# Layer 0's first keys issued ahead of what waits for other transfers, and GpSimd's bias add in the second heads issued behind a key layout

## The chip, the cores and the metric

One core of a Trainium2 chip runs the whole program in one launch. The metric is the device time of one execution in microseconds, as the median of several executions. Engines are named as in the profile: PE is TensorE (PEld its weight load), DVE is VectorE, ACT is ScalarE, POOL is GpSimd, and SP is SyncE, which here only issues transfers. ACT issues transfers too, in order with its own computing.

## The reference

The reference is a chain of four layers on 2048 tokens of width 128 (32 sequences of 64), float32 throughout. Each layer adds a cross attention and then a feed-forward to the residual stream x. Cut to what matters here:

```python
# layer 0, attention: 16 heads of 64; queries from the 64 latents, keys from context and latents
kv_in = concat([layer_norm(ctx, g1, b1), layer_norm(layernorm(x), g2, b2)], axis=1)
q = l @ Wq;  k, v = split(kv_in @ Wkv)
out = softmax(q k^T / 8) v @ Wo;         x = x + out
# layer 0 feed-forward, layer 1 attention, layer 1 mixture of experts (top 2 of 8, two iterations)
# layers 2 and 3, attention: 16 heads of 8 with masks, keys and values from ctx_1024
out = softmax(q k^T / sqrt(8) + mask) v @ Wo + bo;   x = x + out
# layer 2 feed-forward: quantized weights and activations; layer 3: top 2 of 8 experts
```

## The kernel before, in words

**Tiles and groups.** The tokens lie as 16 tiles of 128 in four groups `K.x[g]` of four tiles. Layer 0's attention goes over eight inputs q = 0..7; each holds four batches, with 64 context tokens on partitions 0 to 63 and 64 latents on partitions 64 to 127 (`kv_tok`).

**The folding.** No queries or keys are made. `l0_products` multiplies each head's query and key weights into one 128x128 matrix (`A`, kept as a high and a low part by `take_A`), and the value and output weights into `N`. `l0_project` multiplies the normed latents (`latT`) by `A` in three matmuls per head (`mm3`, L236) into `G`; the scores are then `G` times `kvT` (L445). The products are made in two halves `hf` of eight heads each; projections n = 0..3 need the first half of A, n = 4..7 the second.

**An input's way.** `l0_load` fetches `kv_tok` in two transfers, the context half issued by SP and the latent half by ACT, into two buffers, so the tokens of input q + 2 wait until input q's are read for the last time. `l0_inputs` then runs moments (L154, L155), ln_rs, a power on GpSimd (L161), the normalization (L183), gamma and beta (L403, L404: on VectorE for q = 0, on GpSimd else), four PE transposes (L408), an ACT copy to `kvT` (L409), and splits into high and low parts: `latT_hi` (L213), `latT_lo` (L218), `tokp_hi`, `tokp_lo`. In the code `l0_inputs(1)` and the products come after `l0_inputs(0)`.

**Units.** `l0_unit` takes one (q, tile, half, batch) through scores, softmax, transposes (L465), values (L236 into `c_ps`) and, at the end of a tile, the sum over heads with `N` (L479), which is added to `K.x` (L480). Each unit also makes one projection of the next input. `interleave` keeps three units in flight and, beside them, steps of the tasks in `K.behind`: the weights of the middle layers and each group's further work.

**Who sets the order.** Every engine runs its instructions in the order given. The order is made at build time by a planner that simulates the program with costs of its own and issues what is ready by its clock, in program order where several are. `in_turn` gives it edges that only fix the order of issue of two instructions; `issue_after` does so for all that a block issues on the engine of one instruction. Such an edge brings no waiting of its own between instructions of one engine.

**Constants.** `constants` makes the identity and a column of -0.5; `later_constants`, the first step of the middle weights, makes a bfloat16 and a rounded identity, half of `cols` (all bias columns, one transfer of 24.5 KB, L299), the pair mask and a ranking row. The four loads of `K.x` and the load of `cols` stand in the code after the products.

**The heads of layers 2 and 3.** `heads_xattn(K, i, ...)` runs for i = 0 (layer 2) and i = 1 (layer 3, the second heads). `heads_tile` lays out one tile's keys on GpSimd (`kb`, L1249, two buffers), makes the scores with a mask matmul and a key matmul (L1262, L1263), softmax (L1264 to L1266), transposes (L1273), values (L1283), and at the end of a group turns the output (L204), adds the output bias to `x` on GpSimd (L1309), multiplies by Wo (L1315) and adds to `x` on VectorE (L1316). Three tiles are in flight, so the next group's first tiles are begun before a group's end. For i = 0 the bias add of a group but the last has an edge behind the latest key layout; for i = 1 it has none. `queries` reads x through `hqn` (L183) before the bias may be added. `keep_warm` issues matmuls whose results nobody reads.

Of the kernel before, what the change touches and what calls it, by code (L numbers as in the profile page):

```python
# [4 lines left out]


# [3 lines left out]

# [8 lines left out]
F32 = mybir.dt.float32  # L19
# [5 lines left out]
ALU = mybir.AluOpType  # L25
# [121 lines left out]
def ln_moments(K, pool, xg, own=""):  # L147

    nc = K.nc
    n = xg.shape[1]  # L150
    st = pool.tile([P, n, 6], F32, name="ln_st")
    mv = pool.tile([P, n, 2], F32, name=f"ln_mv{own}")
    for t in range(n):
        nc.vector.bn_stats(st[:, t, :], xg[:, t, :])  # L154
        nc.vector.bn_aggr(mv[:, t, :], st[:, t, :])  # L155
    return mv
# [51 lines left out]
def split(K, pool, src, name, engine=None, bufs=None, after=None):  # L208

    nc = K.nc  # L210
    hi = pool.tile(list(src.shape), F32R, name=f"{name}_hi", bufs=bufs)
    lo = pool.tile(list(src.shape), F32R, name=f"{name}_lo", bufs=bufs)
    first = nc.scalar.copy(hi, src) if isinstance(K, Later) else nc.vector.tensor_copy(hi, src)  # L213
    if after:
        in_turn(K, [after, first])
    if not isinstance(K, Later):
        K.mark = first
    (engine or nc.gpsimd).tensor_tensor(lo, src, hi.bitcast(F32), ALU.subtract)  # L218
    return hi, lo


# [61 lines left out]
def constants(K, pool):  # L283

    nc = K.nc
    K.ident = pool.tile([P, P], F32, name="ident")
    make_identity(nc, K.ident)
    K.neghalf = pool.tile([P, 1], F32, name="neghalf")
    nc.vector.memset(K.neghalf, -0.5)


def later_constants(K, pool):
    nc = K.nc
    K.identb = pool.tile([P, P], BF16, name="identb")
    nc.vector.tensor_copy(K.identb, K.ident)
    K.identr = pool.tile([P, P], F32R, name="identr")
    nc.vector.tensor_copy(K.identr, K.ident)
    K.half = pool.tile([P, NCOL], F32, name="half_cols")
    nc.vector.tensor_scalar(K.half, K.cols, 0.5, None, ALU.mult)  # L299

    K.pair_mask = pool.tile([P, GT, P], BF16, name="pair_mask")
    nc.vector.memset(K.pair_mask, NEG)
    for b in range(2):
        nc.vector.memset(K.pair_mask[b * S : (b + 1) * S, :, b * S : (b + 1) * S], 0.0)

    K.rank = pool.tile([P, 8], F32, name="rank")
    for e in range(8):
        nc.vector.memset(K.rank[:, e : e + 1], float(8 - e))
# [7 lines left out]
N_TAGS = "2n"  # L316


def l0_products(K, out, left, right, hf, tags=("s", "t")):


    ps = [bank(K, tag, [P, 4, P]) for tag in tags]
    for j in range(4):
        for r in range(2):
            rows = slice(r * S, (r + 1) * S)
            K.nc.tensor.matmul(ps[r][:, j, :], left[rows, 4 * hf + j, :], right[rows, 4 * hf + j, :], start=True, stop=True)
    for r in range(2):
        out(ps[r], hf, r)


def l0_xattn(K):


    nc, tc, ins = K.nc, K.tc, K.ins
    with (
        tc.tile_pool(name="l0x_w", bufs=1, reuse_waits="tile") as wp,
        tc.tile_pool(name="l0x_g", bufs=2, reuse_waits="tile") as gp,
        tc.tile_pool(name="l0x_t", bufs=L0_BUFS, reuse_waits="tile") as tp,
    ):
        C = SimpleNamespace(gp=gp, tp=tp, tok={}, keys={}, G={})  # L340

        C.A = tuple(wp.tile([P, 16, P], F32R, name=f"A_{n}") for n in ("hi", "lo"))
        C.N = wp.tile([P, 16, P], F32, name="N")
        with tc.tile_pool(name="first", bufs=1, side="right", reuse_waits="tile") as first:
            l0_load(K, C, 0)
            w = {n: first.tile([P, 8, P], F32, name=n) for n in ("WqT", "WkT", "WvT", "Wo")}
            from_dram = {n: ins[f"L0_xattn_{n}"].rearrange("(c p) d -> p c d", p=P) for n in w}
            half = [slice(4 * hf, 4 * hf + 4) for hf in range(2)]
            gains = wp.tile([P, 2, P], F32, name="gains")
            K.kv_gamma, K.kv_beta = gains[:, 0, :], gains[:, 1, :]  # L350
            for hf in range(2):
                nc.sync.dma_start(w["WqT"][:, half[hf], :], from_dram["WqT"][:, half[hf], :])
                nc.scalar.dma_start(w["WkT"][:, half[hf], :], from_dram["WkT"][:, half[hf], :])
                if hf == 0:
                    nc.sync.dma_start(gains, ins["gains"])
            l0_load(K, C, 1)
            nc.sync.dma_start(w["WvT"], from_dram["WvT"])
            nc.scalar.dma_start(w["Wo"], from_dram["Wo"])
            heads = lambda t, hf, r: t.rearrange("p (c r) d -> p r c d", r=2)[:, r, half[hf], :]

            def take_A(ps, hf, r):
                hi, lo = (heads(a, hf, r) for a in C.A)
                scale = 1.0 / math.sqrt(64.0)
                nc.scalar.activation(hi, ps, AF.Copy, scale=scale)
                nc.vector.scalar_tensor_tensor(lo, ps, scale, hi.bitcast(F32), ALU.mult, ALU.subtract)

            l0_inputs(K, C, 0)
            for hf in range(2):
                l0_products(K, take_A, w["WqT"], w["WkT"], hf)
                for n in range(4 * hf, 4 * hf + 4):  # L370
                    l0_project(K, C, 0, n, "gn"[n % 2])
            l0_inputs(K, C, 1)

            with tc.issue_after(K.projected.ins):
                for hf in range(2):
                    l0_products(K, lambda ps, hf, r: nc.scalar.copy(heads(C.N, hf, r), ps), w["WvT"], w["Wo"], hf, N_TAGS)
        for g in range(NG):
            K.x[g] = K.load(K.const, f"x{g}", [P, GT, P], K.tokens(ins["x"], g))
        K.cols = K.load(K.const, "cols", [P, NCOL], ins["cols"])
        mid_begin(K)  # L380
        units = [(q, t, hf, b) for q in range(8) for t in range(2) for hf in range(2) for b in range(2)]
        interleave(K, (Task(l0_unit(K, C, *u)) for u in units), L0_DEPTH, L0_LAG, L0_RATE)


def l0_load(K, C, q):
    tok = C.tok[q] = C.gp.tile([P, GT, P], F32, name="kv_tok")
    for rows, name, queue in ((slice(0, S), "ctx_1024", K.nc.sync), (slice(S, P), "x", K.nc.scalar)):
        batches = K.ins[name].rearrange("(b s) d -> s b d", s=S)
        queue.dma_start(tok[rows, :, :], batches[:, GT * q : GT * (q + 1), :])


def l0_inputs(K, C, q):

    nc, gp = K.nc, C.gp
    tok = C.tok[q]
    mv = ln_moments(K, gp, tok)
    rs = gp.tile([P, GT], F32, name="ln_rs")
    nc.vector.tensor_scalar(rs[0:S, :], mv[0:S, :, 1], EPS, None, ALU.add)
    nc.vector.tensor_scalar(rs[S:P, :], mv[S:P, :, 1], 1.0 + EPS, EPS * EPS, ALU.mult, ALU.add)
    ln_apply(K, tok, tok, mv, rsqrt(K, gp, rs, "ln_rstd"))  # L400
    full = [P, GT, P]
    engine = nc.vector if q == 0 else nc.gpsimd
    engine.tensor_tensor(tok, tok, K.kv_gamma.unsqueeze(1).to_broadcast(full), ALU.mult)  # L403
    engine.tensor_tensor(tok, tok, K.kv_beta.unsqueeze(1).to_broadcast(full), ALU.add)  # L404
    kvT = gp.tile(full, F32, name="kvT", bufs=3)
    ps = bank(K, "1", full)
    for b in range(GT):
        nc.tensor.transpose(ps[:, b, :], tok[:, b, :], K.ident)  # L408
    nc.scalar.copy(kvT, ps)  # L409
    latp = split(K, gp, kvT[:, :, S : 2 * S], "latT", nc.vector)  # L410
    tokp = split(K, gp, tok, "tokp", bufs=3)
    C.keys[q] = (kvT, latp, tokp)

# [14 lines left out]
def l0_unit(K, C, q, t, hf, b):  # L428
# [5 lines left out]
    G = C.G[q]  # L434
    if n == 0 and q + 2 < 8:
        l0_load(K, C, q + 2)
    if n == 2 and q + 2 < 8:
        l0_inputs(K, C, q + 2)
    if (hf, b) == (0, 0):
# [604 lines left out]
HEAD_BLOCKS = ("L2", "L3")  # L1044
WARM = ((0, 0, 0, 0), (0, 0, 2, 4))
WARM_END = 2


def heads_constants(K, pool):
# [185 lines left out]
def heads_tile(K, C, g, t):  # L1235
# [17 lines left out]
    if C.i:  # L1253
        in_turn(K, [K.l2bo_step, step])
    K.kb_step = step
    yield
    nm = C.gp.tile([P, 16], F32, name="nm", bufs=HX_BUFS)
    e = C.ep.tile([P, 16, S], F32, name="e")
# [50 lines left out]
    step = nc.gpsimd.tensor_tensor(xg, xg, K.hbo[C.i].unsqueeze(1).to_broadcast([P, n, P]), ALU.add)  # L1309
    if C.i == 0 and g < NG - 1:  # L1310
        in_turn(K, [K.kb_step, step])
    yield
    ps = bank(K, QN[C.i], [P, n, P])
    for t in range(n):
# [53 lines left out]
def keep_warm(K, ps, n, after=None):  # L1368

    cols = ps.shape[-1]  # L1370
    moving = K.masks[1].rearrange("p h k -> p (h k)") if len(K.masks[1].shape) == 3 else K.masks[1]
    for _ in range(n):
        step = K.nc.tensor.matmul(ps, K.identb, moving[:, :cols], start=True, stop=True)
        if after is not None:
            in_turn(K, [after, step])
        after = step
    return after
# [361 lines left out]
```

## Time and profile before

| | |
|---|---|
| median of 3 runs | 907.39 us (906.65 to 907.55) |
| the profiled execution, its own time | 907.62 us |
| its span in the profile | 905.9 us |
| PE / DVE / ACT / POOL busy | 821.4 / 732.4 / 563.0 / 328.3 us |
| transfers | 13.73 MB, mean 15 GB/s |

The profile lists busy time, not waiting. A row of the order of time reads: start, duration, engine, line, operation, what it writes and reads, its shape, and in brackets how long the engine was idle before it and what it waited for. DMA queues are SPq and ACTq, by the engine that issues. Matmul durations include a tail that overlaps with the next, so the rate of TensorE is read from the spacing of starts. The windows view gives busy time per engine for stretches of the span.

### The profile page before, as it was taken

How to read it: one execution, taken by the hardware profiler on the slowest of the kernel's cores; microseconds unless marked ns; L12 is line 12 of the kernel's file. 1: busy time of each engine (PE TensorE's matmuls, PEld its weight loads, DVE VectorE, ACT ScalarE, POOL GpSimd, SP SyncE). 2: the span in 40 equal slices, each digit the busy share in tenths (PEclk: the TensorE clock that was granted, in tenths of full speed). 3: DMA queues.
4: the chain of work that ended last, by engine and by line, in shares of the span. 5: the costliest groups of instructions: out<-in, count | busy, mean ns of one | idle time of the engine just before them, and what ended most of it. 6: DMA issues, size and time to landing. Idle time of an engine off the chain costs nothing.

```text
span 905.9 us, 15766 instructions
## 1 busy us (share of the span) xinstructions
PE 821.4 (91%) x5859; PEld 671.2 (74%) x5868; DVE 732.4 (81%) x1877; ACT 563.0 (62%) x1093; POOL 328.3 (36%) x300
## 2 busy tenths in 40 slices
PE   4999999999999988899999799898999779898995
PEld 3989989979988876787787688684676447566663
DVE  5879799798698687877678877789788778789878
ACT  3676685676676599587687768564544484345443
POOL 3764574343243251511040310015474303435342
PEclk9999999999999999999999999999999999899998
DMA  8312000000000000000000000000000000000000
GB/s 191 106 36 59 13 2 12 13 1 1 13 1 1 1 13 0 15 14 21 1 1 1 1 1 1 0 25 1 1 2 1 1 1 1 1 1 1 13 13 24
DMA packets 22670, 13.73 MB, mean 15 GB/s; under 512 B 3009, under 2 KB 21953, under 8 KB 22593
## 3 DMA queue, kind: packets, MB, share of 16 engines
q1 hardware_dynamic: 18320, 10.62, 4.3%
q10 hardware_dynamic: 4272, 2.10, 0.9%
q8 instruction: 46, 0.75, 0.3%
q14 instruction: 32, 0.25, 0.1%
HBM read 11.66 MB, written 1.05 MB: 14 GB/s over the span
## 4 chain that ended last, share of the span: by engine, by line
PE 50%; DVE 25%; ACT 15%; POOL 3%; issue 3%; DMA 2%; SPq 1%; ACTq 0%; DVEq 0%; POOLq 0%
PE c_ps L918 7%; PE g_ps L479 4%; PE s_ps L1263 4%; PE s_ps L445 4%; PE g_ps L236 4%; PE c_ps L236 3%; PE g_ps L1283 2%; PE c_ps L1273 2%; PE s_ps L236 2%; PE t_ps L465 2%; PE t_ps L236 2%; ACT L941 2%; DVE mh_lo L895 1%; ACT L936 1%; DVE m L893 1%
## 5 line engine op out<-in xcount | busy, mean ns | idle before, releaser
L461 POOL TENSOR_TENSOR e<-e,rs 128x512 f32<-128x512 f32 x64 | 67.0, 1058 | 91.7 <-DVE rs L460 52.8
L161 POOL TENSOR_TENSOR ln_rstd<-ln_rs,neghalf 128x4 f32<-128x4 f32 (+1 forms) x38 | 40.8, 1073 | 144.8 <-DVE ln_rs L169 137.5
L1249 POOL TENSOR_TENSOR kb<-hk,head 128x1024 f32<-128x1024 f32 x32 | 63.7, 1993 | 74.2 <-PE s_ps L1263 58.9
L445 PE MATMUL s_ps<-kvT,G 128*128 128x128 f32 x512 | 71.7, 277 | 0.5 <-DVE e L451 0.5
L1263 PE MATMUL s_ps<-kb,hq 128*128 128x512 f32 x128 | 67.3, 609 | 2.1 <-ACT hq L1232 1.9
L445 PEld LDWEIGHTS s_ps<-kvT,G 128*128 128x128 f32 x512 | 65.8, 192 | 4.1 <-DVE e L451 1.9
L918 PE MATMUL c_ps<-mh_hi,w2e_hi 128*128 128x512 f32 x160 | 61.8, 426 | 4.5 <-ACT be L936 2.7
L479 PE MATMUL g_ps<-N,Ct 128*128 128x128 f32 x512 | 62.1, 276 | 1.1 <-ACT G L425 0.7
L479 PEld LDWEIGHTS g_ps<-N,Ct 128*128 128x128 f32 x512 | 60.1, 192 | 2.5 <-ACT G L425 1.3
L1266 ACT ACTIVATE e<-e 128x1024 f32<-128x1024 f32 x32 | 34.0, 1061 | 40.6 <-DVE e L1265 38.1
L1264 DVE TENSOR_REDUCE nm<-s_ps 128x8 f32<-128x512 f32 x64 | 43.7, 683 | 16.0 <-PE s_ps L1263 15.6
L1274 ACT COPY hpT<-c_ps 128x512 f32<-128x512 f32 x64 | 35.1, 589 | 34.2 <-PE c_ps L1273 33.9
L469 DVE TENSOR_TENSOR pT_lo<-t_ps,pT_hi 128x512 fp32r<-128x512 f32 x64 | 43.4, 683 | 13.5 <-ACT pT_hi L468 11.3
L918 PE MATMUL c_ps<-mh_hi,w2e_lo 128*128 128x512 f32 x160 | 51.9, 401 | 0.0
L895 DVE TENSOR_TENSOR mh_lo<-m,mh_hi 128x1024 fp32r<-128x1024 f32 x32 | 40.4, 1263 | 13.9 <-ACT mh_hi L894 12.9
L473 ACT COPY Ct<-c_ps 128x512 f32<-128x512 f32 x64 | 38.4, 600 | 21.2 <-PE c_ps L236 16.4
L918 PE MATMUL c_ps<-mh_lo,w2e_hi 128*128 128x512 f32 x160 | 49.4, 404 | 0.5 <-DVE mh_lo L895 0.5
L425 ACT COPY G<-g_ps 128x512 f32<-128x512 f32 x60 | 35.9, 598 | 21.4 <-PE g_ps L236 18.0
L452 ACT ACTIVATE e<-e 128x512 f32<-128x512 f32 x56 | 35.4, 638 | 20.8 <-DVE e L451 20.5
L1283 PEld LDWEIGHTS g_ps<-hv,hpT 128*64 128x64 f32 x1024 | 33.5, 137 | 19.3 <-issue 7.4
L447 DVE TENSOR_REDUCE nm<-s_ps 128x4 f32<-128x512 f32 x64 | 42.9, 679 | 5.0 <-PE s_ps L445 4.7
L468 ACT CAST pT_hi<-t_ps 128x512 fp32r<-128x512 f32 x64 | 38.1, 598 | 13.3 <-PE t_ps L465 7.3
(524 smaller groups left out, 2651.8 us busy)
## 6 DMA issues: line engine op xcount, KB each, us to landing
kv_tok<-in_x ACTq DMA_DIRECT2D x8, 128.0 KB, 3.3
kv_tok<-in_ctx SPq DMA_DIRECT2D x8, 128.0 KB, 2.9
x<-in_x SPq DMA_DIRECT2D x4, 256.0 KB, 8.3
ctx<-in_ctx SPq DMA_DIRECT2D x4, 256.0 KB, 3.4
w2e_raw<-in_L_ffn_expert_w SPq DMA_DIRECT2D x1, 768.0 KB, 4.4
out<-x SPq DMA_DIRECT2D x3, 256.0 KB, 2.3
WkT<-in_L_xattn_WkT ACTq DMA_DIRECT2D x2, 256.0 KB, 5.3
WqT<-in_L_xattn_WqT SPq DMA_DIRECT2D x2, 256.0 KB, 5.2
```

The lines of the kernel that those rows point to most:

```text
L236: step = K.nc.tensor.matmul(ps, w[a], x[b], start=start and i == 0, stop=stop and i == 2)
L445: nc.tensor.matmul(ps[:, j, :], G[:, bb, h : h + 2, :].rearrange("p h s -> p (h s)"), kvT[:, bb, :], start=True, stop=True)
L447: K.mark = nc.vector.tensor_reduce(nm, ps, AX.X, ALU.max, negate=True)
L461: nc.gpsimd.tensor_tensor(e, e, rs.unsqueeze(2).to_broadcast([P, 4, P]), ALU.mult)
L469: nc.vector.tensor_tensor(lo, ps, hi.bitcast(F32), ALU.subtract)
L479: nc.tensor.matmul(ps, Ct[:, h, :], C.N[:, h, :], start=(h == 0), stop=(h == 15))
L895: nc.vector.tensor_tensor(lo, m, hi.bitcast(F32), ALU.subtract)
L918: nc.tensor.matmul(ps, K.w2p[part][:, 2 * n + i, cols], x[:, i, :, :], start=first, stop=last)
L1249: step = nc.gpsimd.tensor_tensor(kb, K.hk[C.i][g][:, :, t, :].unsqueeze(2).to_broadcast(full), K.head.unsqueeze(1).unsqueeze(3).to_broadca ...
L1263: nc.tensor.matmul(ps, hq[:, half, t, :, :].rearrange("p b s -> p (b s)"), kb[:, half, :, :], start=False, stop=True)
L1264: nc.vector.tensor_reduce(nm[:, heads], ps, AX.X, ALU.max, negate=True)
L1283: values = nc.tensor.matmul(po[b * S : (b + 1) * S, j, :, :].rearrange("p r d -> p (r d)"), pT[:, j, b * S : (b + 1) * S], K.hv[g][:, 2 * ...
```

## The change

In the start:

- the bfloat16 identity and the pair mask are made in `constants`, with the first instructions;
- eight warming matmuls of 128x512 stand first on TensorE, and six more behind the first half of the products, which now comes in the code ahead of `l0_inputs(0)`; the second half of the products is issued behind the last of input 0's transposes (`K.turn0`);
- the moments of input 1 and `half_cols` are issued on VectorE behind input 0's `latT_lo` (`K.lat0`);
- `cols` is loaded ahead of WvT; the four loads of x move into the first unit, behind the tokens of input 2, and both halves of those tokens are issued by SP.

In the heads: for i = 1 each bias add is issued behind the latest second tile's key layout (`C.kb_second`). At the end of group g < 3 that is the second tile of group g + 1, which is already begun; in group 3 it is group 3's own. The warming matmuls take the pair mask as their moving operand everywhere.

```diff
 def split(...):
-    (engine or nc.gpsimd).tensor_tensor(lo, src, hi.bitcast(F32), ALU.subtract)
+    K.split_end = (engine or nc.gpsimd).tensor_tensor(lo, src, hi.bitcast(F32), ALU.subtract)
...
 def later_constants(K, pool):
-    nc.vector.tensor_scalar(K.half, K.cols, 0.5, None, ALU.mult)
+    in_turn(K, [K.lat0, nc.vector.tensor_scalar(K.half, K.cols, 0.5, None, ALU.mult)])
...
 def l0_products(K, out, left, right, hf, tags=("s", "t"), after=None):
+            if after is not None:
+                in_turn(K, [after, step])
...
             l0_load(K, C, 0)
+            keep_warm(K, bank(K, "1", [P, 512]), WARM_START)        # WARM_START = 8
...
             l0_load(K, C, 1)
+            K.cols = K.load(K.const, "cols", [P, NCOL], ins["cols"])
             nc.sync.dma_start(w["WvT"], from_dram["WvT"])
...
+            step = l0_products(K, take_A, w["WqT"], w["WkT"], 0)
+            keep_warm(K, bank(K, "g", [P, 512]), 6, step)
             l0_inputs(K, C, 0)
             for hf in range(2):
-                l0_products(K, take_A, w["WqT"], w["WkT"], hf)
+                if hf:
+                    l0_products(K, take_A, w["WqT"], w["WkT"], hf, after=K.turn0)
...
-        for g in range(NG):
-            K.x[g] = K.load(K.const, f"x{g}", [P, GT, P], K.tokens(ins["x"], g))
-        K.cols = K.load(K.const, "cols", [P, NCOL], ins["cols"])
...
 def l0_load(K, C, q):
-        queue.dma_start(tok[rows, :, :], batches[:, GT * q : GT * (q + 1), :])
+        K.tok_step = (queue if q != 2 else K.nc.sync).dma_start(tok[rows, :, :], batches[:, GT * q : GT * (q + 1), :])
...
 def l0_inputs(K, C, q):
-    mv = ln_moments(K, gp, tok)
+    with K.tc.issue_after(K.lat0.ins) if q == 1 else nullcontext():
+        mv = ln_moments(K, gp, tok)
...
+    if q == 0:
+        K.turn0, K.lat0 = turn, K.split_end
...
 def l0_unit(K, C, q, t, hf, b):
         l0_load(K, C, q + 2)
+        if q == 0:
+            for g in range(NG):
+                x = K.x[g] = K.const.tile([P, GT, P], F32, name=f"x{g}")
+                in_turn(K, [K.tok_step, K.nc.sync.dma_start(x, K.tokens(K.ins["x"], g))])
...
 def heads_tile(K, C, g, t):
+    if t == 1:
+        C.kb_second = step
...
+    if C.i:
+        in_turn(K, [C.kb_second, step])
...
 def keep_warm(K, ps, n, after=None):
-    moving = K.masks[1].rearrange("p h k -> p (h k)") if len(K.masks[1].shape) == 3 else K.masks[1]
+    moving = K.pair_mask.rearrange("p t k -> p (t k)")
```

More of the change, by code (lines that the diff above doesn't have):

```diff
@@ L7 @@
 import math
-from contextlib import ExitStack
+from contextlib import ExitStack, nullcontext
 from types import SimpleNamespace
@@ L287, in constants @@
     make_identity(nc, K.ident)
+    K.identb = pool.tile([P, P], BF16, name="identb")
+    nc.vector.tensor_copy(K.identb, K.ident)
+    K.pair_mask = pool.tile([P, GT, P], BF16, name="pair_mask")
+    nc.vector.memset(K.pair_mask, NEG)
+    for b in range(2):
+        nc.vector.memset(K.pair_mask[b * S : (b + 1) * S, :, b * S : (b + 1) * S], 0.0)
     K.neghalf = pool.tile([P, 1], F32, name="neghalf")
@@ L293, in later_constants @@
     nc = K.nc
-    K.identb = pool.tile([P, P], BF16, name="identb")
-    nc.vector.tensor_copy(K.identb, K.ident)
     K.identr = pool.tile([P, P], F32R, name="identr")
@@ L298, in later_constants @@
     K.half = pool.tile([P, NCOL], F32, name="half_cols")
[L299 to L304, printed above, removed]
+    in_turn(K, [K.lat0, nc.vector.tensor_scalar(K.half, K.cols, 0.5, None, ALU.mult)])
     K.rank = pool.tile([P, 8], F32, name="rank")
@@ L316, with l0_products @@
 N_TAGS = "2n"
-def l0_products(K, out, left, right, hf, tags=("s", "t")):
+def l0_products(K, out, left, right, hf, tags=("s", "t"), after=None):
     ps = [bank(K, tag, [P, 4, P]) for tag in tags]
@@ L325, in l0_products @@
             rows = slice(r * S, (r + 1) * S)
-            K.nc.tensor.matmul(ps[r][:, j, :], left[rows, 4 * hf + j, :], right[rows, 4 * hf + j, :], start=True, stop=True)
+            step = K.nc.tensor.matmul(ps[r][:, j, :], left[rows, 4 * hf + j, :], right[rows, 4 * hf + j, :], start=True, stop=True)
+            if after is not None:
+                in_turn(K, [after, step])
     for r in range(2):
         out(ps[r], hf, r)
+    return step
 def l0_xattn(K):
@@ L407, in l0_inputs @@
     for b in range(GT):
-        nc.tensor.transpose(ps[:, b, :], tok[:, b, :], K.ident)
+        turn = nc.tensor.transpose(ps[:, b, :], tok[:, b, :], K.ident)
     nc.scalar.copy(kvT, ps)
     latp = split(K, gp, kvT[:, :, S : 2 * S], "latT", nc.vector)
+    if q == 0:
+        K.turn0, K.lat0 = turn, K.split_end
     tokp = split(K, gp, tok, "tokp", bufs=3)
@@ L1046 @@
 WARM_END = 2
+WARM_START = 8
 def heads_constants(K, pool):
```

## The prediction

> **What bounds the kernel now.** I read the page first, for the shares; then the chain of waits, to see whether the start is on it; then the order of time of the first 30 us; then stretches of the windows view, for who is full where; last GpSimd's order of time in the second heads.
>
> The page's first lines:
>
> ```profile
> span 905.9 us, 15766 instructions
> PE 821.4 (91%) x5859; PEld 671.2 (74%) x5868; DVE 732.4 (81%) x1877; ACT 563.0 (62%) x1093; POOL 328.3 (36%) x300
> ```
>
> TensorE is the bound on average. Four stretches of the windows view (columns: stretch, span, PE, PEld, DVE, ACT, POOL busy, granted clock, DMA share, GB/s):
>
> ```profile
> 6.40:18.00 11.60, 5.30 (x37) 4.39 (x37) 7.01 (x24) 4.57 (x7) 3.39 (x3) 1.00 1.09 239
> ...
> 25.80:45.00 19.20, 19.11 (x145) 17.42 (x144) 17.53 (x51) 12.22 (x28) 13.57 (x13) 1.00 0.42 124
> ...
> 60.00:260.00 200.00, 195.31 (x1536) 182.11 (x1535) 165.74 (x443) 131.84 (x280) 88.07 (x82) 1.00 0.05 13
> ...
> 782.00:788.00 6.00, 6.00 (x17) 3.11 (x15) 3.06 (x5) 2.23 (x4) 1.91 (x1) 0.59 0.00 0
> ```
>
> Before 18 us TensorE mostly waits while the DMA engines are full. From 25.8 it has no free time, and in the 200 us of layer 0 from 60 on it idles 4.7. Work done earlier at the start should therefore stay gained. VectorE is 91% full from 25.8 to 45, so it can take part of the gain back.
>
> The chain of waits through the start, then VectorE, TensorE and the DMA queue in order of time:
>
> ```profile
> 8.10 3.39 SPq L1593
> ...
> 12.84 3.95 DMA cols<-in_cols
> 16.78 1.16 POOL ln_rstd L161
> ```
> ```profile
> 12.17 0.87 DVE L154 BATCH_NORM_STATS2 ln_st<-kv_tok 128x6 f32<-128x128 f32 x4 [2.93 <-DMA kv_tok<-in_ctx]
> ...
> 12.96 0.67 DVE L404 TENSOR_TENSOR kv_tok<-kv_tok,gains 128x512 f32<-128x512 f32 x1
> ...
> 17.50 0.19 DVE L299 TENSOR_SCALAR half_cols<-cols 128x49 f32<-128x49 f32 x1 [0.51 <-DMA cols<-in_cols]
> 17.61 0.28 DVE L213 CAST latT_hi<-kvT 128x256 fp32r<-128x256 f32 x1
> ...
> 17.95 0.58 PE L236 MATMUL g_ps<-latT_hi,A_hi 128*128 128x256 f32 x1 [3.13 <-DVE latT_hi L213]
> ```
>
> VectorE runs in order. Group 0's beta add (L404) could have started at 9.24, when L403 ended; it stood behind the statistics of group 1, whose tokens landed at 12.17. latT_hi of group 0 could have followed kvT (ready 15.44); it stood behind half_cols, whose cols landed 17.5, because SP issued cols behind four loads of x. The first projection starts at 17.95.
>
> The last thing the start shows is TensorE's rate:
>
> ```profile
> 18.54 0.41 PE L236 MATMUL n_ps<-latT_hi,A_hi 128*128 128x256 f32 x1
> 18.75 0.41 PE L236 MATMUL n_ps<-latT_hi,A_lo 128*128 128x256 f32 x1
> ...
> 27.63 0.28 PE L236 MATMUL g_ps<-latT_hi,A_lo 128*128 128x256 f32 x1
> 27.75 0.28 PE L236 MATMUL g_ps<-latT_lo,A_hi 128*128 128x256 f32 x1
> ```
>
> That row is one form: starts 0.21 us apart at 18.5, 0.12 apart at 27.6. The granted clock column reads 1.00 in both, so the first 26 us must be judged by spacing. All 48 projections of group 0 ran slow: 48 x 0.096 = 4.6 us too much.
>
> **The change, part by part.**
>
> *Edits with one answer.* identb and pair_mask among the first constants: both were already made by 3.38, cost 0. The masks operand of the warming matmuls in the heads has the same width and type: 0. Saved handles for ordering issue nothing.
>
> *Eight warming matmuls at the front.* The nearest row is 128x512 bf16 in the hidden layer (L1461, starts 0.215 apart at full rate); by 0.213/0.117 that is 0.39 slow, up to 0.43 at half rate, so 3.1 to 3.4 us from 3.4 to 6.5-6.8. The first products began at 6.42 waiting for WkT: delay 0 to 0.4. Products last 2.0 (6.42 to 8.46), so they end near 8.9. The six after them cost 1.3 fast or 2.6 slow: TensorE is free at 10.2 to 11.5. The kv tokens are ready at 9.9, or 11.2 if the two A_lo (0.66 each) go first. Transposes start at 10.2 to 11.5, against 13.73.
>
> *When the rate rises.* In this trace work went on without a break over 0.1 us from 19.47, and the spacing changed between 25.6 and 27.4: 6 to 8 us of work. From 3.4 that is 9.5 to 11.5, before the first projection. *The skill* (TensorE: Matmul & The Clock Gate, Part 1) says a busy free-running window of about 3.4 us does it, so an estimate by it is 6.9 to 10.3; that changes only how fast the six run. The same section speaks against the change: the ramp is under 1% of a typical span and not worth fitting. Here 4.6 of 907 us is indeed 0.5%, but that is over twice what this measurement can tell apart.
>
> *First keys.* Transposes at 10.8 (middle), 0.60 to 1.09 long, kvT copy 0.58, latT_hi 0.28, with some 0.3 of hand-overs: first projection near 12.7, 5.2 earlier. The second half's products (1 to 2 us) lie under the copy and the splits.
>
> *Where this stops.* Group 1's statistics now stand behind latT_lo (ends about 13.4). Then in line: statistics 0.87+0.36, two A_lo 1.35, half_cols 0.19, ln_rs 0.33, GpSimd's power 1.16, apply 1.12, GpSimd's gains 1.38+1.28, to 21.5; before, the gains ended at 21.90. So group 1's normalization hardly moves. What moves is what followed: its transposes waited for slow matmuls until 23.66 and latT_hi for VectorE until 26.34. Without both: transposes 0.60, copy 0.59, latT 0.28, hops 0.3, first projection of group 1 at about 23.3 against 27.43: 4.1 earlier, 5.4 if the A_lo go behind the statistics. In the time before it TensorE has 48 x 0.12 = 5.8 us of projections, three score groups of 0.46 and all four N products of 1.09, 11.6 us for the 10.6 from 12.7 to 23.3. Three of the four N products ran after 27.43 before, another 3.3 us credited, if TensorE binds.
> Bounds: 8.7 gained (5.4+3.3); or VectorE binds: it had done 4.2 us by 19.41 that now is still to do at 13.4, so 6.0-4.2 = 1.8. I take 5.2, nearer the key chain than the credit, because VectorE is 91% full to 45.
>
> *Transfers.* cols (24.5 KB, issue 0.83) goes ahead of WvT on SP; WvT landed 13.7 and is first read at 25.87 (now 15 to 18 at the earliest): 0. The x loads (four issues, 6.50 us of SP at full DMA load) now wait behind tokens of group 2, which wait on SP for group 0's slot (tokp_lo, some 14 us). Queued behind on SP: wf, later tokens (25.59 before) and weights; x is first added at 59.7. Hidden by 35 us. ACT is freed of one issue that stood in its order at 17.74 (0.60). Without x, 1 MB of 2.6 MB leaves the full stretch: 0 to 1 us for group 1's tokens, which no longer bind.
>
> *GpSimd's bias add in the second heads.* Its order of time, and TensorE:
>
> ```profile
> 773.13 1.27 POOL L1309 TENSOR_TENSOR x<-x,hbo 128x512 f32<-128x512 f32 x1 [0.93 <-DVE hqn L183]
> 775.59 1.02 POOL L161 TENSOR_TENSOR ln_rstd<-ln_rs,neghalf 128x4 f32<-128x4 f32 x1 [1.19 <-DVE ln_rs L169]
> 777.32 0.76 POOL L1309 TENSOR_TENSOR x<-x,hbo 128x256 f32<-128x256 f32 x1 [0.72 <-DVE hqn L183]
> 778.04 1.90 POOL L1249 TENSOR_TENSOR kb<-hk,head 128x1024 f32<-128x1024 f32 x1
> ```
>
> Five adds run as soon as hqn has been read (754.89 to 780.10), long before use. The key layout at 778.04 stands behind one; its buffer was free at 776.67. Gain at most 1.3, and it may lie under VectorE, for which TensorE waited 1.83 at 781.27. The adds land after the layouts of 785.84, 803.35 and 832.59; the outputs that need them are at 801.09, 830.62 and 863.71, cover 12 us or more. But at 805.35 and 836.40 a power sits on GpSimd for the last feed-forward: an add ahead costs 1.27, or 1.27+0.76+0.72 = 2.75 with the halves. Range -1.3 to +4.0; I take -0.5, since both powers come 0.1 us or more behind their layouts' end only if adds are put between.
>
> *The order itself.* A planner with its own costs orders the program again. Nearest row: one mishap of order is the 1.83 idle plus the half-rate stretch behind it, about 2.4 us, 4.2 in all. Bounds -4.2 to +4.2, taken 0.
>
> Sum against the profiled execution, 907.62 (span 905.9 and 1.7 around it): -5.2 -0.5 = -5.7, 901.9. The median is 0.2 lower: **901.8**.
>
> **The rivals.** *The gain is taken back (no change), 0.11*: VectorE binds up to 45 and only 1.8 remains, with 0 to 1.3 lost in the tail: 905.6 to 906.9. For it: 91% VectorE; against: 1.7 us VectorE idle in that stretch and 2.8 at 45 to 60. *The tail turns (slower), 0.11*: both adds stand ahead of the powers (+4.0), TensorE waits and falls to half rate at each, as at 782 to 788 (2.4 each): 8.8 against 5.2 gained, 911.2. It decides once both happen; one alone (1.27+2.4) still leaves the kernel faster. *The change warms but does not advance the keys, 0.15 within faster*: A_lo and late planning hold kvT back to 13.7, leaving the 3 to 4.6 of rate: 903 to 905. *All credits, 0.15 within faster*: 8.7 and 1.3: 897.6.
>
> **How the numbers follow.** What a measurement here can tell from no change is 0.2%, 1.8 us. Faster: 0.48 for the forecast and 0.30 in two variants, 0.78; same 0.11; slower 0.11. The range takes in full credit, 897.0, and the small-gain cases up to 907.0.
>
> **What would show it.** First projection near 12.7 and spacing 0.12 from there; group 1's first projection at 22 to 24; no half_cols wait; TensorE full from 12.7 to 45; the chain's start without x and cols; adds behind 785, 803 and 832 in the old time. Wrong if group 1 still begins after 26, if layer 0's attention ends within 2 us of before, or if powers wait for adds in the tail.

## The result, and the profile after

The changed kernel takes 911.79 us (median of 17 runs), the kernel before 907.02 us (17 runs): a ratio of 1.0043, 95% interval 1.0029 to 1.0057. It is slower by 0.43%, where 0.6% faster was forecast. The profiled execution took 911.40 us; before, 907.62. Ratios and intervals, here and below, are set against executions of the kernel before in the same session; executions of one kernel spread over some 4 to 11 us, and the ratio is not exactly the quotient of two medians.

The page's first lines, then the windows view of the same kernel (stretch, span, then PE, PEld, DVE, ACT and POOL busy, granted clock, DMA share, GB/s):

```profile
span 909.7 us, 15802 instructions
PE 826.7 (91%) x5874; PEld 671.4 (74%) x5882; DVE 735.8 (81%) x1877; ACT 563.6 (62%) x1093; POOL 328.1 (36%) x300
```
```profile
6.40:18.00 11.60, 10.35 (x87) 8.17 (x86) 6.60 (x21) 6.91 (x13) 1.98 (x2) 1.00 0.80 176
18.00:21.00 3.00, 0.51 (x5) 0.30 (x4) 1.63 (x7) 0.00 (x0) 0.00 (x0) 1.00 0.79 226
21.00:25.80 4.80, 4.80 (x26) 4.45 (x27) 4.38 (x16) 1.17 (x2) 3.58 (x4) 0.64 0.40 116
25.80:45.00 19.20, 17.08 (x126) 14.89 (x125) 18.16 (x46) 12.84 (x29) 12.39 (x12) 1.00 0.43 124
45.00:60.00 15.00, 12.19 (x89) 10.72 (x90) 14.92 (x30) 8.07 (x16) 12.86 (x10) 1.00 0.19 53
60.00:260.00 200.00, 194.51 (x1512) 180.50 (x1511) 166.91 (x439) 131.78 (x282) 87.81 (x81) 1.00 0.05 13
```

Up to 18 us the forecast holds: TensorE is busy for 10.35 us of 11.60, where it was 5.30. Then comes a hole. From 18 to 21 TensorE works for 0.51 us, GpSimd and ScalarE not at all; from 21 to 25.8 the granted clock is 0.64; from 25.8 to 45 TensorE idles 2.1 us where it idled 0.1, and from 45 to 60 it idles 2.8 where it idled 0.9, while VectorE has no free time.

The order of time at the start shows first what went as forecast:

```profile
3.44 3.60 PE L1392 MATMUL c_ps<-pair_mask,identb 128*128 128x512 bf16 x8 [3.44 <-DVE identb L289]
...
12.09 0.36 PE L236 MATMUL g_ps<-latT_hi,A_hi 128*128 128x256 f32 x1
12.28 0.29 PE L236 MATMUL g_ps<-latT_hi,A_lo 128*128 128x256 f32 x1
```

The first projection starts at 12.09, 5.9 us earlier than before, and the next ones follow 0.12 apart. Now VectorE, TensorE and GpSimd in order of time through the hole:

```profile
19.36 0.87 DVE L154 BATCH_NORM_STATS2 ln_st<-kv_tok 128x6 f32<-128x128 f32 x4 [5.20 <-DMA kv_tok<-in_x]
20.14 0.67 DVE L370 SCALAR_TENSOR_TENSOR A_lo<-t_ps,A_hi 128x512 fp32r<-128x512 f32 x1
20.73 0.15 DVE L405 TENSOR_SCALAR ln_rs<-ln_mv 64x4 f32<-64x4 f32 x1
...
20.87 0.39 PE L236 MATMUL g_ps<-latT_hi,A_lo 128*128 128x256 f32 x1 [2.49 <-DVE A_lo L370]
...
21.14 1.99 POOL L161 TENSOR_TENSOR ln_rstd<-ln_rs,neghalf 128x4 f32<-128x4 f32 x2 [9.62 <-DVE ln_rs L406]
...
26.75 2.50 POOL L411 TENSOR_TENSOR kv_tok<-kv_tok,gains 128x512 f32<-128x512 f32 x2
...
31.54 0.36 PE L236 MATMUL g_ps<-latT_hi,A_hi 128*128 128x256 f32 x1
```

The same places in the kernel before: input 2's statistics, the end of input 1's gains, input 1's first projection.

```profile
21.45 0.87 DVE L154 BATCH_NORM_STATS2 ln_st<-kv_tok 128x6 f32<-128x128 f32 x4 [2.03 <-DMA kv_tok<-in_ctx]
...
20.62 1.28 POOL L404 TENSOR_TENSOR kv_tok<-kv_tok,gains 128x512 f32<-128x512 f32 x1
...
27.43 0.36 PE L236 MATMUL g_ps<-latT_hi,A_hi 128*128 128x256 f32 x1
```

Input 1's statistics were done at 14.16 in the changed kernel. The next VectorE instruction is the statistics of input 2, for whose tokens VectorE stands 5.20 us. Behind it, in VectorE's order, wait the last A_lo of the first input's matrices and input 1's own ln_rs. Neither needs input 2. TensorE runs out of projections and waits 2.49 us for that A_lo. Input 1's power comes at 21.14, 4.4 us later than in the kernel before (16.77). And since input 2's moments are now done too, the "x2" rows show GpSimd taking both inputs in turns: input 1's gains end at about 28, where they ended at 21.90 before. Input 1's first projection comes at 31.54 instead of 27.43.

The DMA queue of SP says why the tokens were late:

```profile
8.29 1.77 SPq L1612 DMA_DIRECT2D w_r<-in_L_ffn_w_r  x2
...
10.93 2.89 SPq L674 DMA_DIRECT2D w_h<-in_L_ffn_w_h  x4
14.75 0.50 SPq L697 DMA_DIRECT2D bs<-in_cols  x1
15.38 0.60 SPq L394 DMA_DIRECT2D kv_tok<-in_ctx  x1
16.02 0.61 SPq L394 DMA_DIRECT2D kv_tok<-in_x  x1
```

Their slot was free at 11.53 (GpSimd's tokp_lo, its last reader, ran from 10.25 for 1.28). SP was issuing small expert weights until 15.25. That is no worse than before, when the same loads stood ahead of these tokens and they went out at 18.32. What is new is who waits: in the kernel before, input 2's statistics stood on VectorE behind input 1's normalization and latT_lo, and waited 2.03 us there, at 21.45, with only the later splits of input 1 behind them (tokp_hi at 23.01, latT_hi at 26.34).

How far each instruction moved against the kernel before, worked out from both traces as the median difference of the starts of the same instructions, sorted by their start in the kernel before: -7.3 us between 20 and 30, -4.8 between 30 and 40, -3.5 between 40 and 50, -0.5 between 50 and 60, +1.9 between 70 and 80. The advance of the start is spent by 60 us.

### The profile page after: what moved, and what is told of

Same layout as the page of the kernel before. It is cut to its first block, busy times and chain, and to the rows that moved or that the text cites. A ratio compares the mean times of both kernels' runs of the same rounds, so it can differ in the third digit from the quotient of the medians.

```text
span 909.7 us, 15802 instructions
## 1 busy us (share of the span) xinstructions
PE 826.7 (91%) x5874; PEld 671.4 (74%) x5882; DVE 735.8 (81%) x1877; ACT 563.6 (62%) x1093; POOL 328.1 (36%) x300
## 4 chain that ended last, share of the span: by engine, by line
PE 47%; DVE 28%; ACT 15%; issue 3%; POOL 3%; DMA 2%; SPq 0%; ACTq 0%; DVEq 0%; POOLq 0%
PE c_ps L932 6%; PE s_ps L1280 4%; PE g_ps L493 4%; PE s_ps L459 4%; PE c_ps L236 3%; PE g_ps L236 3%; PE g_ps L1300 2%; PE c_ps L1290 2%; PE s_ps L236 2%; PE t_ps L236 2%; PE t_ps L479 2%; ACT L955 2%; ACT L950 1%; DVE kv_tok L183 1%; DVE mh_lo L909 1%
```

## The experiments

Two theories. **The wait**: the start is worth what was forecast, and input 2's moments ahead of input 1's work take it back, by the wait and by what the interleaving sets off. **The heads**: the start is worth less because VectorE is full, and the bias adds in the second heads cost the rest.

**Each part alone.** The first kernel is the changed one without the late edge, the second the kernel before with only that edge.

```diff
 # start only
-    if C.i:
-        in_turn(K, [C.kb_second, step])
 # heads only (in the kernel before)
+    if t == 1:
+        C.kb_second = step
...
+    if C.i:
+        in_turn(K, [C.kb_second, step])
```

> The changed kernel without the edge that puts the second heads' bias add behind a key layout; the start as changed. Theory A (the start loses by itself: VectorE stands 5.2 us for the tokens of input 2, and the kernel is 2.4 us behind before by 70 us and stays so to 800 us; the heads lose another 1.4): 910.3, half the tail's loss of 1.4 below the changed kernel or more, and 2 to 4 above before. Rival B (all of the loss is in the heads and the start comes out even): 907 to 908.

> The kernel before with that edge alone. Theory A: slower than before by the 1.4 us that the two traces differ after 800 us, 908.4. Rival B: slower by 4 or more. Rival C (the edge is neutral, the 1.4 us is the phase of the clock in one profile): 906.5 to 907.5.

Measured: the start alone 909.17 us, ratio 1.0017 (1.0004 to 1.0031); the heads alone 908.71 us, 1.0001 (0.9981 to 1.0020). So the start by itself brings no gain but a small loss, 1.5 us (2.1 by the medians, nearer to theory A's 2 to 4 than to rival B's even start), and of the edge by itself nothing can be told from zero: its median lies at theory A's 908.4, its ratio at rival C's nothing. The two together are slower than either; the pairs further down take that up.

**The tokens sooner.** The nine small loads go behind input 2's tokens on SP. VectorE's order in the start stays that of the changed kernel.

```diff
+            K.tok2 = K.tok_step
...
-    K.w_r1 = K.load(...)          # w_r2, w_h2, w_h1 likewise
+    with K.K.tc.issue_after(K.K.tok2.ins):
+        K.w_r1 = K.load(...)
...
-        nc.sync.dma_start(K.bs1[half, :], ...)
+        in_turn(K.K, [K.K.tok2, nc.sync.dma_start(K.bs1[half, :], ...)])
```

> The changed kernel, with the nine small expert loads (w_r, w_h, bs) ordered on SP behind input 2's tokens, so that these are issued at about 11.6 instead of 15.4 and land near 15.5. VectorE's order through the start is that of the changed kernel. Theory A (the wait costs what it lasts): VectorE waits about 1.3 instead of 5.2 us, input 1's ln_rs comes 3.9 us earlier, and 3 to 4 us come back: 908 to 909. Rival D (the loss is in VectorE and GpSimd getting in each other's way between 30 and 60 us, where VectorE is full; the wait only precedes it): under 1.5 us come back, 910.3 to 912.

Measured: 906.72 us, 0.9989 (0.9969 to 1.0009). VectorE's order of time:

```profile
15.79 0.87 DVE L154 BATCH_NORM_STATS2 ln_st<-kv_tok 128x6 f32<-128x128 f32 x4 [1.73 <-DMA kv_tok<-in_x]
```

The wait fell from 5.20 to 1.73 us and the time by 0.54% (1.0043 to 0.9989), 4.9 us, more than theory A's 3 to 4. In the two traces the same instructions lie 3.6 us earlier from 20 to 70 and 2.2 to 3.8 earlier from there to the end: about the 3.47 us by which the wait shrank, kept through the whole program. So the wait is shown to be part of the cause. But input 1's first projection still comes at 27.96, no earlier than before the change (27.43), with GpSimd still taking inputs 1 and 2 in turns. This kernel is not told apart from the one before.

**Input 2's moments behind input 1's normalization.** An edge on VectorE alone; SP's queue up to input 2's tokens stays as it is in the changed kernel. The second kernel has this and the tokens sooner.

```diff
-    with K.tc.issue_after(K.lat0.ins) if q == 1 else nullcontext():
+    with K.tc.issue_after((K.lat0 if q == 1 else K.applied).ins) if q in (1, 2) else nullcontext():
         mv = ln_moments(K, gp, tok)
...
-    ln_apply(K, tok, tok, mv, rsqrt(K, gp, rs, "ln_rstd"))
+    K.applied = ln_apply(K, tok, tok, mv, rsqrt(K, gp, rs, "ln_rstd"))
```

> The changed kernel, with input 2's moments issued on VectorE behind input 1's normalization instead of ahead of its ln_rs. Transfers as in the changed kernel: the tokens still land near 19.3. Theory A: input 1's ln_rs near 15.5 instead of 20.7, its power on GpSimd near 16, its gains finished near 21 instead of 29; first projection of input 1 before 25; 3 to 6 us come back: 906 to 909. Rival D: under 1.5 us come back, 910.3 to 912.

> Input 2's moments behind input 1's normalization, and the nine small expert loads behind input 2's tokens on SP. Theory A (what counts is when input 1's keys are ready, 25 to 27 us there already): the remaining wait of 2.2 us for the tokens goes, input 2's keys come up to 3 earlier, TensorE uses part of it: 898.5 to 900.5. Rival (a second wait as dear as the first): 897 or less. Rival (TensorE is full, nothing is left): 900.6 within 0.8.

Measured: 900.60 us, 0.9925 (0.9897 to 0.9953), and with both edits 900.38 us, 0.9918 (0.9893 to 0.9942). The first is a larger return than theory A's 906 to 909; the second fits theory A and the rival of a full TensorE alike. The order of time of the first, VectorE, GpSimd, TensorE (a profiled execution of 906.53 us, the slowest of nine; it is read for its start, not for its total):

```profile
16.39 1.11 DVE L183 TENSOR_SCALAR kv_tok<-kv_tok,ln_mv,ln_rstd 128x128 f32<-128x128 f32 x4 [1.13 <-POOL ln_rstd L161]
19.66 0.87 DVE L154 BATCH_NORM_STATS2 ln_st<-kv_tok 128x6 f32<-128x128 f32 x4 [2.16 <-DMA kv_tok<-in_x]
...
18.94 1.28 POOL L411 TENSOR_TENSOR kv_tok<-kv_tok,gains 128x512 f32<-128x512 f32 x1
...
25.38 0.36 PE L236 MATMUL g_ps<-latT_hi,A_hi 128*128 128x256 f32 x1
```

The tokens still land at 19.66 and VectorE still waits for them, 2.16 us. But input 1 has passed by then: its gains end at 20.22 and its first projection comes at 25.38 (24.67 with both edits). So it is not the wait as such that costs, but what stands behind it. Where the tokens-sooner kernel had 0.9989, these have 0.64% and 0.71% less (by the intervals, give or take 0.3%): that much more is lost with the two inputs in turns, even when the wait is short. The advance now lasts: with both edits the median shift against the kernel before is -8.8 us between 30 and 40 and still -7.3 between 100 and 110.

Where this second part is lost can be read too. Against the tokens-sooner kernel the one with both edits is 0.9 us ahead between 30 and 40, 5.0 between 50 and 60 and 6.1 between 70 and 80. The windows from 40 to 60, and VectorE's normalization of input 3, first with the tokens sooner, then with both edits:

```profile
40.00:60.00 20.00, 16.17 (x116) 14.09 (x117) 18.69 (x35) 12.71 (x27) 17.85 (x14) 1.00 0.15 41
...
40.49 3.96 DVE L183 TENSOR_SCALAR kv_tok<-kv_tok,ln_mv,ln_rstd 128x128 f32<-128x128 f32 x4
```
```profile
40.00:60.00 20.00, 19.60 (x153) 17.96 (x153) 16.66 (x46) 13.72 (x29) 17.41 (x13) 1.00 0.16 49
...
35.91 1.11 DVE L183 TENSOR_SCALAR kv_tok<-kv_tok,ln_mv,ln_rstd 128x128 f32<-128x128 f32 x4
```

With the inputs in turns VectorE is busy 18.69 us of 20 with 35 instructions, against 16.66 with 46, and TensorE works 3.4 us less. Input 3's normalization takes 3.96 us, mostly beside GpSimd's work (39.48 to 43.85), against 1.11 with GpSimd idle (35.70 to 37.15). That is the place and the mechanism that rival D named. It holds for this second part, not for the first, which came back with the tokens. The rows are of single executions, and no run takes away this slowing alone, so its share is argued, not shown.

**Only GpSimd's turns.** The tokens-sooner kernel, with input 2's first gain issued on GpSimd behind input 1's second.

```diff
+    if q == 2:
+        in_turn(K, [K.gained, step])      # step: the gamma product
```

> The kernel with the tokens first, and input 2's first gain on GpSimd issued behind input 1's second, which there stood interleaved (input 1's gains ended 3 to 4 us after they could have). VectorE's order through the start stays. Theory A: input 1's keys come 1.3 to 3 us earlier, 904 to 905.5. Rival D (VectorE is full from 30 to 60 us and paces): 906.7 within 1.

Measured: 909.44 us, 1.0022 (0.9998 to 1.0047), a miss. Input 1's gains now end at 23.39 instead of 24.42, but the planner ordered other engines anew around the edge. On TensorE three score groups, an N product and input 2's transposes come ahead of input 1's first projection, which starts at 32.17 instead of 27.96. And two inputs later VectorE's wait comes back, input 4's statistics ahead of input 3's normalization:

```profile
40.10 0.49 DVE L154 BATCH_NORM_STATS2 ln_st<-kv_tok 128x6 f32<-128x128 f32 x2 [3.73 <-DMA kv_tok<-in_x]
```

This kernel does not isolate GpSimd's turns, then; its last row is a second sight of the wait. How the 0.64 to 0.71% divides between GpSimd's queue and VectorE's stays open.

**The warming alone.** The kernel with input 2's moments behind input 1's normalization, without the fourteen warming matmuls in the start.

```diff
-            keep_warm(K, bank(K, "1", [P, 512]), WARM_START)
...
-            keep_warm(K, bank(K, "g", [P, 512]), 6, step)
```

> Input 2's moments behind input 1's normalization, without the fourteen warming matmuls. The planner orders VectorE a little differently from input 1 on. If the rate of the 48 first projections is on the path (4.6 us, as the prediction counted it): 904 to 905.5. If input 1's normalization paces the start, so that slow projections lie under it: 900 to 902.

Measured: 905.75 us, 0.9968 (0.9950 to 0.9985), against 0.9925 with them: 0.43%, 3.9 us, with intervals that just touch. TensorE's order of time without them:

```profile
14.67 0.41 PE L236 MATMUL g_ps<-latT_hi,A_lo 128*128 128x256 f32 x1
14.88 0.41 PE L236 MATMUL g_ps<-latT_lo,A_hi 128*128 128x256 f32 x1
...
16.20 0.28 PE L236 MATMUL g_ps<-latT_hi,A_lo 128*128 128x256 f32 x1
16.32 0.28 PE L236 MATMUL g_ps<-latT_lo,A_hi 128*128 128x256 f32 x1
...
27.29 0.66 PE L413 MATMUL c_ps<-ident,kv_tok 128*128 128x128 f32 x4 [1.41 <-POOL kv_tok L409]
28.79 0.97 PE L457 MATMUL s_ps<-kvT,G 128*128 128x128 f32 x4 [0.85 <-ACT e L468]
29.41 0.56 PE L236 MATMUL g_ps<-latT_hi,A_hi 128*128 128x256 f32 x1
```

Only the first ten projections or so are 0.21 apart, not 48: 1 us of rate, and 0.85 us by which the first projection is later (13.22 against 12.37). For the rest the trace shows a changed order. Input 1's first projection comes at 29.41, 4.0 us later than with the warming (25.38): on TensorE it now stands behind input 2's transposes, which wait 1.41 us for GpSimd, and behind scores that wait 0.85. The granted clock from 25.8 to 45 is 0.91 in this profile, where it is 1.00 with the warming. So 3.9 us is the worth of the warming with the order that the planner made beside it, not of the matmuls' rate; the rate's part was not isolated.

**The late edge, in pairs.** Does the edge explain the difference between 1.0043 and 1.0017? Five more runs without or with it, four of them two pairs on one chip:

> Input 2's moments behind input 1's normalization, without the edge in the second heads. If the edge costs what it cost between the changed kernel and the start alone (0.26%, 2.4 us): 898 to 899. If it is neutral, as between before and the edge alone: 900 to 901.5.

> The changed kernel itself once more, beside the next three on one chip, to settle what the second heads' edge is worth. Edge worth nothing (the two kernels that differ only by it in the late stage, and before with and without it, showed no difference): ratio to before 1.002 to 1.005, and within 0.15% of its twin without the edge. Edge costs (rival, from 1.0043 against 1.0017 on two chips): 0.2 to 0.3% above its twin.

> The changed kernel without the second heads' edge, on the same chip as its twin. Edge worth nothing: ratio 1.002 to 1.005, as its twin. Edge costs: 0.2 to 0.3% below its twin, 1.000 to 1.003.

> Input 2's moments behind input 1's normalization and the small expert loads behind input 2's tokens, without the second heads' edge. Edge worth nothing: 0.990 to 0.994, as its twin with the edge (0.9918 on another chip). Edge costs: 0.2 to 0.3% below its twin.

> The same with the second heads' edge, on the same chip. Edge worth nothing: 0.990 to 0.994 and within 0.15% of its twin. Edge costs: 0.2 to 0.3% above its twin. If the cause of the loss is as told (a wait for input 2's tokens ahead of input 1's work, and what it sets off on GpSimd), this kernel is 0.010 to 0.014 below the changed one on the same chip.

| start | without the edge | with the edge |
|---|---|---|
| as before | 1 | 1.0001 (0.9981 to 1.0020) |
| changed, first session | 1.0017 (1.0004 to 1.0031) | 1.0043 (1.0029 to 1.0057), another session |
| changed, one chip | 1.0018 (0.9999 to 1.0038) | 1.0043 (1.0025 to 1.0061) |
| moments behind input 1 | 0.9933 (0.9910 to 0.9957) | 0.9925 (0.9897 to 0.9953), another session |
| both edits, one chip | 0.9948 (0.9925 to 0.9971) | 0.9916 (0.9892 to 0.9940) |

With the changed start the edge costs 0.25% twice, as the rival said beforehand (0.2 to 0.3%); with the mended starts the kernel with it is 0.1 and 0.3% faster, and both of these pairs missed both of their expectations. In each single pair the intervals overlap. The edge has no price of its own that holds for every start; with the changed start its cost came twice and alike, so that of the 0.43% some 0.17 is the start's and 0.26 goes with the edge. On the one chip, mending the start is worth 1.27% with the edge (1.0043 to 0.9916) and 0.70% without (1.0018 to 0.9948): 11.5 and 6.3 us; the 0.010 to 0.014 written down beforehand for the first was met with 0.0127. That is the cost of the order, and it is there whatever the edge does.

What the edge does to the order is plain. GpSimd's order of time in the changed kernel:

```profile
807.61 1.27 POOL L1326 TENSOR_TENSOR x<-x,hbo 128x512 f32<-128x512 f32 x1
808.84 1.02 POOL L161 TENSOR_TENSOR ln_rstd<-ln_rs,neghalf 128x4 f32<-128x4 f32 x1
```

The add stands ahead of the power, as the slower rival had it, and so do others at 832.19 and 834.11. From the layout at 805.74 to the last one, at 854.86, 49.12 us pass; in the kernel before it is 47.39 (803.35 to 850.74). It is 49.1 in all eight profiles with a changed start and the edge, and 47.2 to 47.4 in the five without it. But it is 47.37 in the heads-only kernel, which has the same adds ahead of the same power. There the order of TensorE in this stretch is the same too; what differs is how long its clock stays low after a wait for VectorE of 1.8 us. Windows of the heads-only kernel and of the changed kernel run again, around that wait:

```profile
839.00:846.30 7.30, 6.62 (x27) 4.54 (x26) 4.37 (x14) 1.53 (x3) 0.09 (x1) 0.77 0.13 37
```
```profile
843.80:852.90 9.10, 8.43 (x28) 5.63 (x27) 4.40 (x15) 1.53 (x3) 0.02 (x1) 0.62 0.10 30
```

Nearly the same matmuls take 7.30 us at a mean clock of 0.77, and 9.10 us at 0.62. In the order of time the half rate lasts from 839.8 to about 843.0 in the one and from 844.7 to about 852.5 in the other. These are single profiled executions; that such a difference decides the pairs above is argued, not shown.

## Why the prediction was wrong

**What failed is the step "Where this stops".** It is the step of the start: without the edge the start was to give 5.2 us and cost 1.5, while the heads' -0.5 came as +2.4, inside its stated -1.3 to +4.0. The step wrote down VectorE's line from latT_lo to input 1's gains: statistics, two A_lo, half_cols, ln_rs, the power, the apply, the gains, "to 21.5". Input 2's statistics are missing from that line. The same text moved the tokens of input 2 in its *Transfers* term, and there it asked only what is queued behind them on SP (x, hidden by 35 us, which was right) and not who waits for them. The trace of before had the row that bore on it, 2.03 us of VectorE standing for these tokens at 21.45, and the edge held back only input 1's moments, so nothing kept input 2's out of the gap. Priced as it came, the wait is 5.20 us on VectorE at a place where input 1 and TensorE stand behind it, and input 1's gains ended at about 28, not 21.5.

**The order term was too small.** "One mishap of order" was bounded by 4.2 us either way and taken as 0. The mishap cost 6.3 to 11.5 us, because it is not one stall: with the edge, 4.9 us went with most of the wait, and another 5.8 to 6.4 (0.64 to 0.71%) with the order of two inputs in turns behind it.

**The gain of the start was of the right size, in another kernel.** With the order mended and no late edge the two kernels give 0.9933 and 0.9948, 6.1 and 4.7 us, against the 5.2 of the sum; with the edge 6.8 to 7.6. In the changed kernel the first projection came at 12.09 (12.7 forecast) and the spacing was 0.12 from there. Part of that is luck: WkT landed late, so the first products began at 7.99 instead of 6.4 to 6.8, but they ran at the full rate and took 1.2 us instead of 2.0. The forecast for input 1's first projection, 22 to 24, was met nearly, at 24.67, once both edits were in. That is 2.8 us earlier than before, not 4.1, while the whole kernel gained more than that, so the agreement with 5.2 does not confirm the sum term by term. "VectorE takes part of it back" was rightly weighed as a rival. In the best kernel it is not what happened: VectorE is 18.6 of 19.2 us busy from 25.8 to 45, and the gain stays. In the changed kernel something like it did: VectorE is 14.9 of 15.0 us busy from 45 to 60 and TensorE idles 2.8, and by 60 us the advance is gone. But the rival had VectorE bound up to 45 by its amount of work, and here it is longer at the same instructions.

**The smaller terms.** half_cols waits for nothing now (13.11, forecast so). The warming was put at 4.6 us and measured 3.9, but that with another order, and only some 1.8 of it can be read as rate and earlier start. The estimate that the rate rises after 6 to 8 us of work was too long: in the changed kernel the first products, at 7.99, already follow each other 0.11 apart in pairs, after 3.60 us of warming and a pause of 0.96. *The Trainium skill* (TensorE: Matmul & The Clock Gate, Part 1) gives about 3.4 us, which is nearer to this trace; it also puts the ramp under 1% of a typical span and advises not to fit it, and the 0.43% that went with the warming here is under 1% and was still measurable.

**The heads.** -0.5 was taken within -1.3 to +4.0. Nothing that can be measured came of the edge alone in the kernel before. The slower rival's mechanism, adds ahead of the powers, is in the trace, and beside the changed start 0.25% or so (2.3 us) went with it, well under the 8.8 that the rival had for the tail; why the same order costs nothing in the heads-only kernel stays open. None of the rivals named what lost the start.

**The signs that were named beforehand** worked: "wrong if group 1 still begins after 26" is the row that failed first (31.54), and it points at the right 15 us of the trace.

## What to carry to other kernels

When work is moved ahead on an engine that runs in order, write out that engine's whole new line, with every instruction whose input may be ready by the planner's clock, and ask of each what lands last for it; a transfer must be priced by who stands waiting for it and what is queued behind, not only by what follows it on its own queue. An edge that holds back the next input leaves the one after it free to take its place, so hold that back too: here the best kernel needed one more edge of the same kind, and the nine small loads out of the tokens' way, for 900.4 us and 899.2 us in two sessions (0.9918 and 0.9916), faster than both the kernel before and the changed one. Where a planner orders the program, an edge added to mend one wait can make the same wait elsewhere.

## What the runs showed of the hardware

A short wait can cost TensorE more than its length, and not the same each time: after waits of 1.8 and 0.7 us the same sequence of matmuls ran at half rate for 3.2 us in one profile and 7.8 us in another, and after the 2.49 us at 20.87 for some 4 us. The Trainium skill (TensorE: Matmul & The Clock Gate, Part 1) calls the window that decides the change of clock free-running, so that the point of change depends on where in it the first matmul lands, and gives a spread of 500 ns from run to run. The two lengths here differ by 4.6 us, so that spread does not account for them, and no run here varied the phase alone.

VectorE is slowed beside GpSimd: in the changed kernel the normalization of four tiles (L183) that takes 1.11 us at 7.14, with GpSimd idle, takes 3.96 us at 44.07, while GpSimd runs tensor_tensor instructions without a pause (43.06 to 47.44). The tokens-sooner kernel shows the same, 3.96 us at 40.49.
